# Attention and expert FFN on one core: the attention steps spread over fewer expert tiles

## The chip, the core and the metric

One core of one Trainium2 chip. The metric is the device time of one execution in microseconds; the time before is 1267.89 us, the median of three runs (1267.0 to 1276.63).

## The reference

x has 8 sequences of 1024 tokens with 256 features. After a layernorm two branches are computed from the same xn and both are added to x, all in float32.

```python
xn = layernorm(x)
# causal linear attention, 16 heads of 16
q, k, v = (xn @ W.T split into heads for W in (Wq, Wk, Wv))
q, k = elu(q) + 1, elu(k) + 1
out = einsum('blhd,blhde->blhe', q, cumsum(k (x) v, axis=1))
den = clip(einsum('blhd,blhd->blh', q, cumsum(k, axis=1)), 1e-6)
attention = (out / den).reshape(B, L, 256) @ Wo.T
# mixture of 8 experts, the best 2 for each token
c = softmax over the 2 highest of (xn @ Wr + br), zero elsewhere
ffn = sum over e of c[e] * ((silu(xn @ W1[e]) * (xn @ W3[e])) @ W2[e])   # hidden size 512
return x + attention + ffn
```

## The kernel before

**Attention** works on 16 blocks of 512 tokens, each cut into 4 chunks of 128. `block_steps(t)` is a generator that gives the work of one block in 9 steps, counted from 0: steps 0 to 3 project q, k and v, transpose k, and take the sums for the denominator (`project`; the matmuls den, and at the end eight rden copies on SP's queue); step 4 computes the scores of chunk 0 (`scores`, tile s_ps) and finishes the block before with `attend`; steps 5 to 8 take one chunk each: `carry` and `weigh` (tile o_ps, then oT on DVE) and, for the chunk before, `attend` (the projection a_ps by Wo on PE, and the copy at on ACT). The last block has a tenth step, which finishes its fourth chunk. That makes LAST = 145 steps.

`attend` adds a block's result to out in DRAM with an accumulating DMA on POOL's queue, one of 512 KB for a block (L1001). For the last block there are two (L999): 384 KB with chunks 0 to 2 once the third is copied, and 128 KB with the fourth.

**The experts' FFN** works on 132 tiles of 128 token-and-expert pairs (j from 0 to 131; NM = 132). Tiles 0 to 24 add to acc_d, which is copied into out after tile 26, the others add to out (out_dram in the profile). For each tile:

- `ffn_load` gathers the token rows xg and the table row entry by two indirect DMAs on POOL's queue, five tiles ahead.
- `ffn_norm` (ACT) and `ffn_halves` (DVE) prepare the rows, and `ffn_turn_halves` turns them by a transposing DMA on SP's queue (halfT), `ffn_join` (ACT) makes xgT of it.
- `ffn_weights(j + 2)` loads W1 and W3 of the tile's expert, 2 x 512 KB on SP's queue, into five buffers.
- `ffn_hidden` computes both halves of gu_ps (L1265, PE), the silu on ACT (L1273) and the product hT on DVE (L1276).
- `ffn_out(j - 1)` computes y_ps of the tile before (L1284, PE) and scales it to y on DVE (L1291). The y tiles have five buffers.
- `ffn_store` adds y to out by an indirect accumulating DMA on POOL's queue (L1295).

Every accumulating DMA into out waits for the one before it to land, since the framework keeps writes to the same DRAM tensor in order, and POOL issues them in its own order, the gathers between them.

**What sets the order.** The main loop goes over j. In each turn it first lets `attend_upto(n)` make attention steps until n are made, and then calls `ffn_step(j)`. n grows with j: slowly up to tile 22 (READ), and from there evenly up to the end, so that attention lies between the FFN tiles on PE. `attend_upto` makes one step in a turn, and a further one only if that is step 0, 4 or 8 of a block (TOGETHER). From what is then in program order a scheduler makes each engine's order; the DMAs on SP's queue, and PE's matmuls in the last tile, keep program order.

```python
        else:
            attend_upto(AHEAD + (LAST - 1 - AHEAD) * (j - READ + 1) // (NM - 1 - READ) + j // (NM - 1))
        ffn_step(j, LATE if N1 < j <= N1 + LATE else 0)
```

Here AHEAD = 23 and LAST = 145. At j = 130 the first 144 steps are done, and the last one comes at j = 131.

Of the kernel before, what the change touches and what calls it, by code (L numbers as in the profile page):

```python
# [64 lines left out]
def tile_attention_moe(  # L65
# [33 lines left out]
    NM = NF - NR  # L99
# [46 lines left out]
    def load_x(t, queue):  # L146
        xbs[t] = f_x.tile([P, NCH, H], F32, tag="xb", name=f"xb{t}")
        in_order(queue.dma_start(out=xbs[t], in_=xf[t]))
# [123 lines left out]
    def moments(t, n):  # L272


        def small(name, *shape, dtype=F32):
            return f_two.tile([P, n * NCH, *shape], dtype, tag=name, name=name)

        less, rstd = (tab[:, t * NCH : (t + n) * NCH, w] for w in (1, 2))
        st = small("st", 6)
        mv = small("mv", 2)  # L280
        for c in range(n * NCH):
            nc.vector.bn_stats(st[:, c, :], xbs[t + c // NCH][:, c % NCH, :])
            nc.vector.bn_aggr(mv[:, c, :], st[:, c, :])
        v = small("v")
        nc.vector.tensor_scalar(v, mv[:, :, 1], EPS_NORM, None, ALU.add)
        if t <= FB:
            nc.gpsimd.tensor_tensor(rstd, v, neg_half, ALU.pow)
        else:

            half = small("half")  # L290
            nc.vector.tensor_scalar(half, v, -0.5, None, ALU.mult)
            bits = small("bits", dtype=I32)
            nc.vector.tensor_scalar(bits, v.bitcast(I32), 1, None, ALU.arith_shift_right)
            nc.vector.tensor_scalar(bits, bits, -1.0, float(0x5F3759DF), ALU.mult, ALU.add)
            y = bits.bitcast(F32)
            for i in range(4):
                sq = small("sq")
                nc.vector.tensor_tensor(sq, y, y, ALU.mult)
                nc.vector.tensor_tensor(sq, sq, half, ALU.mult)
                y_new = small(f"y{i % 2}") if i < 3 else rstd  # L300
                nc.vector.scalar_tensor_tensor(y_new, sq, 1.5, y, ALU.add, ALU.mult)
                y = y_new
        yield
        nc.vector.scalar_tensor_tensor(less, mv[:, :, 0], -1.0, rstd, ALU.mult, ALU.mult)
        yield

    def normalise(t):
        xb = xbs.pop(t)
        less, rstd = (tab[:, t * NCH : (t + 1) * NCH, w] for w in (1, 2))
        for c in range(NCH):  # L310
            if t < FB and (c % 2 == 0 or t == FB - 1):
                nc.vector.tensor_scalar(
                    xb[:, c, :], xb[:, c, :], rstd[:, c : c + 1], less[:, c : c + 1],
                    ALU.mult, ALU.add,
                )
            else:
                nc.scalar.activation(
                    xb[:, c, :], xb[:, c, :], AF.Identity, bias=less[:, c : c + 1],
                    scale=rstd[:, c : c + 1],
                )  # L320
        scaled[t] = xb

    def turn(t):
        xn = scaled.pop(t)
        if 0 < t < FB:
            xnT = e_one.tile([P, KC, TB], F32, name=f"xnT{t}")
        else:
            xnT = (two if t == 0 else f_two).tile([P, KC, TB], F32, tag="xnT", name="xnT")
        for k in range(KC):
            tp = ps_t.tile([P, TB], F32, tag="t", name="tp")  # L330
            for c in range(NCH):
                done = nc.tensor.transpose(  # L332
                    tp[:, bass.ts(c, P)], xn[:, c, bass.ts(k, P)], ident
                )
                if t == FB + 1:
                    in_order(done)
            nc.scalar.copy(xnT[:, k, :], tp)
        turned[t] = xnT
        if t == 0:
            turned_first.append(xnT)  # L340
        elif t != FB - 1:
            store(t)
# [19 lines left out]
    def add_logits(t, n, tp):  # L362
        a = t % ROUND
        if a == 0:
            lgs[t] = f_two.tile([P, ROUND * NCH, E], F32, tag="lg_all", name="lg_all")
        nc.vector.tensor_tensor(
            lgs[t - a][:, a * NCH : (a + n) * NCH, :],
            tp.rearrange("p (c e) -> p c e", e=32)[:, :, 0:E],
            br_sb.unsqueeze(1).to_broadcast([P, n * NCH, E]), ALU.add,
        )  # L370
# [664 lines left out]
    LAST = NBLK * STEPS + 1  # L1035
# [11 lines left out]
    def attend_upto(n, apart=True):  # L1047
        first = True
        while steps_made[0] < min(n, LAST):
            if apart and not first and steps_made[0] % STEPS not in TOGETHER:  # L1050
                break
            next(steps)
            steps_made[0] += 1
            first = False
# [117 lines left out]
    def ffn_load(j):  # L1172
        table, _, num_i, src_i, _, _, i = of_tile(j)
        xg[j] = ffn4.tile([P, H], F32, tag="xg", name="xg")
        rows = nc.gpsimd.indirect_dma_start(  # L1175
            out=xg[j], out_offset=None, in_=x_rows[:, :],
            in_offset=bass.IndirectOffsetOnAxis(ap=src_i[:, i : i + 1], axis=0),
        )
        entry[j] = ffn8.tile([P, 3], F32, tag="entry", name="entry")
        nc.gpsimd.indirect_dma_start(  # L1180
            out=entry[j], out_offset=None, in_=table[:, :],
            in_offset=bass.IndirectOffsetOnAxis(ap=num_i[:, i : i + 1], axis=0),
        )
        return rows

    def ffn_norm(j):
        in_order(
            nc.scalar.activation(  # L1188
                xg[j], xg[j], AF.Identity, bias=entry[j][:, 1:2], scale=entry[j][:, 2:3]
            )  # L1190
        )
# [3 lines left out]
    def ffn_halves(j):  # L1195

        halves[j] = ffn2.tile([P, 2, H], U16, tag="half", name="half")
        nc.vector.tensor_copy(  # L1198
            halves[j], xg.pop(j).bitcast(U16).rearrange("p (h b) -> p b h", b=2)
        )  # L1200
# [102 lines left out]
    def ffn_step(j, behind):  # L1303


        while loaded[0] < min(NM, j + (5 if j >= READ else 4)):
            ffn_load(loaded[0])
# [29 lines left out]
    LATE = 3  # L1337
    LISTS = NBLK - FB
    READ = LISTS + 10
    AHEAD = 2 + LISTS // 2 + 3 * (READ - LISTS) // 2  # L1340
    for j in range(NM + 1):
        if j + 1 < TURNED:
            ffn_norm(j + 1)
        if TURNED <= j + 2 < NM:
            ffn_norm(j + 2)
            ffn_halves(j + 2)
        t = FB + j
        counting = FB < t <= NBLK and t % ROUND == 0
        if counting and t == NBLK:
            for _ in routing:  # L1350
                pass
        if 0 < j and t < NBLK:
            if j % 2 == 0:
                with tc.issue_after((last_token if j < 4 else last_masked)[0].ins):
                    for _ in moments(t, 2):
                        pass
            normalise(t)
            turn(t)
            if t + 5 < NBLK:
                load_x(t + 5, nc.scalar)  # L1360
            add_logits(t, 1, logits_turned(t))
            if (t + 1) % ROUND == 0:
                routing = route(t + 1 - ROUND, t + 1)
                next(routing)
        if j == LISTS:
            in_order(
                nc.sync.dma_start(
                    out=tab_d[1][1 : 1 + NS * P, :].rearrange("(p i) w -> p (i w)", p=P),
                    in_=tab.rearrange("p i w -> p (i w)"),
                )  # L1370
            )
            in_order(nc.sync.dma_start(out=tab_d[1][0:1, :], in_=before[0:1, 0:3]))
            lists = second_batch(taken)
        if LISTS <= j < READ:
            next(lists)
        if LISTS <= j < LISTS + NBLK - FB:
            t = FB + j - LISTS
            rows = slice(t * TB, (t + 1) * TB)
            in_order(nc.sync.dma_start(out=out_rows[rows, :], in_=x_rows[rows, :]))
        if j < LISTS:  # L1380
            attend_upto(3 + j // 2)
        elif j < READ:
            attend_upto(AHEAD - 3 * (READ - j - 1) // 2)
        else:
            attend_upto(AHEAD + (LAST - 1 - AHEAD) * (j - READ + 1) // (NM - 1 - READ) + j // (NM - 1))
        ffn_step(j, LATE if N1 < j <= N1 + LATE else 0)
        if counting and j < LISTS:
            for _ in routing:
                pass
        if j == N1 + 1:  # L1390
            copied.append(j)
            in_order(nc.sync.dma_start(out=out_rows[0 : FT * P, :], in_=acc_d[:, :]))
# [54 lines left out]
```

## Time and profile before

| what | value |
|---|---|
| median of three runs | 1267.89 us |
| the profiled execution, its own time | 1267.09 us |
| its span, from the first to the last instruction | 1265.3 us |
| PE (TensorE matmul) busy | 1217.8 us, 96% of the span |
| PEld (TensorE weight load) busy | 1057.0 us, 84% |
| DVE (VectorE) busy | 676.0 us, 53% |
| ACT (ScalarE) busy | 557.1 us, 44% |
| POOL (GpSimd) busy | 519.9 us, 41% |
| moved by DMA | 245.84 MB, 194 GB/s in the mean |
| granted TensorE clock, mean | 0.991 |

PE and PEld are two parts of one engine that overlap. Starts are in microseconds from the begin of the span. A line such as `L1295 POOL DMA_INDIRECT out_dram<-y,dst_i` names the line of the kernel, the engine, the operation, and the tile written from the tiles read; in brackets stands how long the engine had been idle before it, and what that idle time is put down to. For POOL's DMAs the duration is that of the issue, not of the transfer. A wait for several things is put down to the one that came last by the profile, and "issue" means that nothing the profile shows was waited for.

### The profile page before, as it was taken

What the parts mean: (1) busy time and instruction counts of PE and PEld (TensorE: products, weight loads), DVE (VectorE), ACT (ScalarE), POOL (GpSimd) and SP (SyncE); (2) the same over time, 40 slices, a digit from 0 to 9 for tenths busy, and PEclk for the clock granted to TensorE, in tenths of its full rate; (3) what the DMA queues carried; (4) which work ended last, traced back from release to release, by engine and by line L of the source; (5) the groups of instructions that cost most, each with busy time, mean ns of one, the idle gap of its engine ahead of it and who ended that gap; (6) DMA issues with size and microseconds to landing.
All of it is one profiled execution on the core that took longest, in us unless ns stands there. A gap on an engine that the chain in (4) does not pass through costs nothing.

```text
span 1265.3 us, 29694 instructions
## 1 busy us (share of the span) xinstructions
PE 1217.8 (96%) x11434; PEld 1057.0 (84%) x11434; DVE 676.0 (53%) x1541; ACT 557.1 (44%) x1062; POOL 519.9 (41%) x460
## 2 busy tenths in 40 slices
PE   5899999999999999999999999999999999999995
PEld 3577887787898998888888889989888889899884
DVE  7767589863354454545454544545453544545451
ACT  4565465461433526262623426162625344262620
POOL 3643233233344544443435444443544444443422
PEclk9999999999999999999999999999999999999997
DMA  9897565557788697969789897979897787969782
GB/s 329 289 288 242 168 189 119 187 155 208 206 201 194 165 235 164 225 173 211 168 194 203 164 234 155 223 181 192 185 206 171 198 202 170 216 154 231 167 176 35
DMA packets 203678, 245.84 MB, mean 194 GB/s; under 512 B 72674, under 2 KB 127586, under 8 KB 203250
## 3 DMA queue, kind: packets, MB, share of 16 engines
q1 hardware_dynamic: 160146, 189.65, 52.2%
q0 software_dynamic: 38064, 43.27, 24.5%
q10 hardware_dynamic: 5328, 11.01, 2.4%
q8 instruction: 94, 1.54, 0.5%
q14 instruction: 46, 0.38, 0.1%
HBM read 187.91 MB, written 44.29 MB: 184 GB/s over the span
## 4 chain that ended last, share of the span: by engine, by line
PE 86%; DVE 6%; DMA 3%; ACT 2%; issue 1%; POOL 1%; SPq 0%; POOLq 0%; DVEq 0%; ACTq 0%
PE gu_ps L1265 36%; PE y_ps L1284 16%; PE s_ps L911 6%; PE o_ps L948 5%; PE a_ps L990 4%; PE zq L794 4%; PE zkv L810 4%; PE zkk L810 4%; PE o_ps L930 2%; PE tp L332 1%; PE tp L857 1%; DMA halfT<-half 1%; PE lg_ps L355 1%; DVE at_place L572 1%; PE den L879 1%
## 5 line engine op out<-in xcount | busy, mean ns | idle before, releaser
L1265 PE MATMUL gu_ps<-xgT,w 128*128 128x128 f32 x4224 | 507.8, 278 | 1.2 <-DVE s_sb L918 0.8
L1265 PEld LDWEIGHTS gu_ps<-xgT,w 128*128 128x128 f32 x4224 | 488.0, 192 | 19.9 <-issue 13.5
L1295 POOL DMA_INDIRECT out_dram<-y,dst_i x107 | 175.5, 1640 | 338.4 <-DVE y L1291 72.9
L1284 PE MATMUL y_ps<-w_sb,hT 128*128 x1056 | 250.9, 381 | 1.8 <-DVE hT L1276 1.6
L1175 POOL DMA_INDIRECT xg<-in_x_dram,src_i x132 | 128.3, 972 | 230.5 <-DVE half L1198 99.0
L1284 PEld LDWEIGHTS y_ps<-w_sb,hT 128*128 128x128 f32 x1056 | 190.9, 191 | 23.2 <-DVE hT L1276 2.0
L918 DVE TENSOR_TENSOR s_sb<-s_ps,causal 128x512 f32<-128x512 f32 x256 | 159.9, 683 | 86.8 <-PE s_ps L911 76.8
L1273 ACT ACTIVATE hT<-gu_ps 128x512 f32<-128x512 f32 x132 | 78.8, 597 | 284.5 <-PE gu_ps L1265 279.8
L1276 DVE TENSOR_TENSOR hT<-gu_ps,hT 128x512 f32<-128x512 f32 x132 | 90.4, 685 | 64.9 <-PE gu_ps L1265 36.6
L1180 POOL DMA_INDIRECT entry<-tab_d,of_i x107 | 105.9, 990 | 42.3 <-issue 31.7
L1198 DVE COPY half<-xg 128x512 uint16<-128x512 uint16 x105 | 47.9, 457 | 132.4 <-ACT xg L1188 132.4
L1291 DVE TENSOR_SCALAR y<-y_ps,entry 128x256 f32<-128x256 f32 x132 | 63.7, 483 | 101.5 <-PE y_ps L1284 101.4
L995 ACT COPY at<-a_ps 128x256 f32<-128x256 f32 x64 | 23.7, 371 | 169.5 <-PE a_ps L990 127.0
L911 PE MATMUL s_ps<-qm,kT 32*128 32x256 f32 x1024 | 89.0, 405 | 1.7 <-DVE hT L1276 1.6
L1216 ACT COPY xgT<-halfT 128x512 uint16<-128x512 uint16 x105 | 79.7, 760 | 4.9 <-DMA halfT<-half 4.8
L1188 ACT ACTIVATE xg<-xg,entry 128x256 f32<-128x256 f32 x132 | 78.8, 598 | 3.6 <-DMA entry<-tab_d,num_i 3.6
L990 PE MATMUL a_ps<-wo_sb,oT 128*128 128x256 f32 x256 | 68.4, 389 | 3.0 <-DVE oT L965 2.8
L948 PE MATMUL o_ps<-s_sb,va 128*32 128x128 f32 x2048 | 70.7, 278 | 0.0
L911 PEld LDWEIGHTS s_ps<-qm,kT 32*128 32x128 f32 x1024 | 51.8, 184 | 20.9 <-issue 10.7
L948 PEld LDWEIGHTS o_ps<-s_sb,va 128*32 128x32 f32 x2048 | 52.8, 110 | 18.1 <-issue 15.5
L1295 POOL DMA_INDIRECT acc_d<-y,src_i x25 | 41.2, 1649 | 53.1 <-DVE y L1291 18.0
L794 PE MATMUL zq<-xnT,wq_sb 128*128 128x512 f32 x128 | 60.3, 613 | 0.3 <-DVE s_sb L918 0.3
(215 smaller groups left out, 1343.9 us busy)
## 6 DMA issues: line engine op xcount, KB each, us to landing
w<-in_w_dram SPq DMA_DIRECT2D x264, 512.0 KB
rden<-over SPq DMA_DIRECT2D x128, 64.0 KB
xnT_d<-xnT ACTq DMA_DIRECT2D x15, 512.0 KB
xnT<-xnT_d SPq DMA_DIRECT2D x15, 512.0 KB
out_dram<-at POOLq DMA_DIRECT2D x13, 512.0 KB
out_dram<-in_x_dram SPq DMA_DIRECT2D x12, 512.0 KB
xb<-in_x_dram SPq DMA_DIRECT2D x10, 512.0 KB
w_sb<-in_w_dram SPq DMA_DIRECT2D x4, 1024.0 KB
```

Source lines behind the costliest of these rows:

```text
L794: nc.tensor.matmul(z, lhsT=wq_sb[:, k, bass.ts(o, P)], rhs=xnTs[t][:, k, :], start=(k == 0), stop=(k == KC - 1),)
L810: nc.tensor.matmul(z[:, i, :], lhsT=xnTs[t][:, k, bass.ts(c + i, P)], rhs=wkv_sb[:, k, a, :], start=(k == 0), stop=(k == KC - 1),)
L911: nc.tensor.matmul(s_ps[r][:, hh].rearrange("p a l -> p (a l)"), lhsT=kT[rows, hh, span], rhs=qm[rows, hh, :, span], start=True, stop=True,)
L918: last_masked[0] = nc.vector.tensor_tensor(sm, s_ps[r].rearrange("p k a l -> p (k a) l"), causal_b, ALU.mult)
L948: nc.tensor.matmul(o_ps[32 * r : 32 * r + 32, hh, :], lhsT=va[:, c, 4 * hh + r, a, :], rhs=s_sb[r][:, 2 * hh + a, :], start=(first and a = ...
L990: nc.tensor.matmul(a_ps, lhsT=oT[:, hh, :], rhs=wo_sb[:, hh, :], start=(hh == 0), stop=(hh == 1),)
L1175: rows = nc.gpsimd.indirect_dma_start(out=xg[j], out_offset=None, in_=x_rows[:, :], in_offset=bass.IndirectOffsetOnAxis(ap=src_i[:, i : i ...
L1180: nc.gpsimd.indirect_dma_start(out=entry[j], out_offset=None, in_=table[:, :], in_offset=bass.IndirectOffsetOnAxis(ap=num_i[:, i : i + 1], ...
L1265: done = nc.tensor.matmul(ps[:, i, :], lhsT=w13[:, k, bass.ts(i, P)], rhs=xgT[j][:, k, :], start=(k == 0), stop=(k == KC - 1),)
L1276: nc.vector.tensor_tensor(hT, gu[1], hT, ALU.mult)
L1284: done = nc.tensor.matmul(y_ps, lhsT=hT[:, i, :], rhs=w2_sb[:, bass.ds(e * (IC * H) + i * H, H)], start=(i == 0), stop=(i == IC - 1),)
L1295: nc.gpsimd.indirect_dma_start(out=rows[:, :], out_offset=bass.IndirectOffsetOnAxis(ap=dst_i[:, i : i + 1], axis=0), in_=ys.pop(j), in_off ...
```

## The change

The number of attention steps wanted after tile j reaches its end at j = END = 127 instead of 131. The step count for each tile from 22 on is spread over 105 tiles instead of 109. The last step (the fourth chunk of the last block) is due at tile 127 or 128 at the latest; by the counts of the new formula it is made at 127, and tiles 128 to 131 have no attention step. The addition of the last block in two parts (L999) stays as it is.

```diff
     READ = LISTS + 10
+    END = NM - 5
     AHEAD = 2 + LISTS // 2 + 3 * (READ - LISTS) // 2
...
         else:
-            attend_upto(AHEAD + (LAST - 1 - AHEAD) * (j - READ + 1) // (NM - 1 - READ) + j // (NM - 1))
+            spread = (LAST - 1 - AHEAD) * (min(j, END) - READ + 1) // (END - READ)
+            attend_upto(AHEAD + spread + j // (END + 1))
         ffn_step(j, LATE if N1 < j <= N1 + LATE else 0)
```

Tiles up to 28 have the steps that they had. From 29 on a step comes at the same tile or up to four tiles earlier: block 15 begins at tile 120 instead of 123, its weighing of chunk 3 is at tile 126 instead of 130, and its last step at 127 instead of 131.

## The prediction

> **What bounds the kernel now.** I read the page first, then the windows by stage, then the timeline of the end and of POOL alone. The page:
>
> ```profile
> span 1265.3 us, 29694 instructions
> PE 1217.8 (96%) x11434; PEld 1057.0 (84%) x11434; DVE 676.0 (53%) x1541; ACT 557.1 (44%) x1062; POOL 519.9 (41%) x460
> PEclk9999999999999999999999999999999999999997
> ```
>
> The share of 96% is a mean. By stages (columns: window, its length, busy time of PE, PEld, DVE, ACT, POOL, then granted clock, DMA share, GB/s):
>
> ```profile
> 350.00:500.00 150.00, 148.78 (x1392) 132.01 (x1391) 74.50 (x137) 64.16 (x109) 68.00 (x56) 1.00 0.86 195
> 500.00:650.00 150.00, 150.00 (x1425) 132.61 (x1424) 73.06 (x134) 62.62 (x108) 66.43 (x55) 1.00 0.81 186
> 650.00:800.00 150.00, 150.00 (x1459) 134.12 (x1458) 74.03 (x138) 62.78 (x106) 65.73 (x55) 1.00 0.88 196
> 1100.00:1240.00 140.00, 140.00 (x1339) 124.26 (x1338) 67.32 (x124) 58.32 (x98) 51.84 (x41) 1.00 0.77 173
> 1240.00:1250.40 10.40, 9.55 (x59) 8.35 (x57) 2.13 (x4) 0.97 (x2) 2.56 (x2) 1.00 0.39 52
> 1250.40:1265.30 14.90, 0.01 (x1) 0.00 (x0) 0.48 (x1) 0.00 (x0) 3.16 (x2) 0.57 0.23 26
> ```
>
> PE is full from 350 us to 1240 us at clock 1.00 (the windows left out are full as well); the one hole is 1.22 us near 386 us. So where attention stands between the tiles costs nothing there, and moving it gains nothing. Then PE ends at 1250.41 and 14.9 us follow without it. The timeline of the end, all engines, shows what fills them:
>
> ```profile
> 1248.41 2.00 PE L1284 MATMUL y_ps<-w_sb,hT 128*128 x8 [0.85 <-DVE hT L1276]
> 1249.06 0.91 POOL L999 DMA_DIRECT2D out_dram<-at  x1 [2.74 <-DMA out_dram<-y,dst_i]
> 1250.44 0.48 DVE L1291 TENSOR_SCALAR y<-y_ps,entry 128x256 f32<-128x256 f32 x1 [2.09 <-PE y_ps L1284]
> 1253.58 1.62 POOL L1295 DMA_INDIRECT out_dram<-y,dst_i  x1 [3.61 <-DMA out_dram<-at]
> 1258.07 1.54 POOL L1295 DMA_INDIRECT out_dram<-y,dst_i  x1 [2.87 <-DMA out_dram<-y,dst_i]
> ```
>
> Every addition into out_dram waits until the one before it has landed, and they leave in POOL's order. The last tile's y is in memory at 1250.92 but leaves at 1258.07: its turn comes 7.66 us after PE's end. From there to the end of the span it is 7.2 us, whatever happens. The end is set by this chain of additions, not by PE. Further back on POOL:
>
> ```profile
> 1211.98 1.40 POOL L1001 DMA_DIRECT2D out_dram<-at  x1 [4.37 <-DMA out_dram<-y,dst_i]
> 1222.56 1.65 POOL L1295 DMA_INDIRECT out_dram<-y,dst_i  x1 [9.18 <-issue]
> 1227.82 1.55 POOL L1295 DMA_INDIRECT out_dram<-y,dst_i  x1 [3.62 <-DVE kv L977]
> 1232.37 1.56 POOL L1295 DMA_INDIRECT out_dram<-y,dst_i  x1 [2.99 <-DMA out_dram<-y,dst_i]
> 1237.92 1.35 POOL L999 DMA_DIRECT2D out_dram<-at  x1 [4.00 <-issue]
> 1244.67 1.65 POOL L1295 DMA_INDIRECT out_dram<-y,dst_i  x1 [5.40 <-issue]
> ```
>
> Read the starts as steps of the chain. Quiet memory: 128 KB take 4.39, 4.52 and 4.49 us (the three last), 384 KB take 6.75 us (1237.92 to 1244.67). With weights in flight: 128 KB take 5.26 us (1222.56 to 1227.82) or 5.95 us (from the store at 1206.03 to 1211.98), 512 KB take 10.58 us (1211.98 to 1222.56); over all blocks a 512 KB addition takes 8.7 to 13.2 us to the next one.
>
> **The change, part by part.** No instruction is added or removed. Counting the steps out, block 15 moves three to four tiles earlier: its fourth chunk's scores are weighed at tile 126 and its last projection (a_ps) is done ahead of tile 127, where it was in the midst of 131. Earlier blocks slide by 0 to 3 tiles; the first difference is at tile 29.
>
> Middle, tiles 29 to 127: the same PE work in the same order of blocks, its 121 steps spread over 105 tiles instead of 109. In the old run blocks 4 to 6 make steps 3 and 4 apart, blocks 7 to 11 together, and both lie in the windows that are full. Cost 0, covered by PE; DVE at 73 of 150 us and ACT at 64 have room.
>
> At tile 29 two queues are passed. On POOL the addition of block 2 (L1001, 512 KB) now goes ahead of the stores of y 25 and y 26, which went first. The old rows there:
>
> ```profile
> 371.82 1.44 POOL L1001 DMA_DIRECT2D out_dram<-at  x1 [2.29 <-issue]
> 383.69 1.62 POOL L1295 DMA_INDIRECT out_dram<-y,dst_i  x1 [8.44 <-DMA out_dram<-at]
> 390.77 1.80 POOL L1295 DMA_INDIRECT out_dram<-y,dst_i  x1 [4.02 <-DMA out_dram<-y,dst_i]
> ```
>
> L1001 should start near 365 (the old den matmuls at 361.7, then scores and a_ps with 2.3, copy and issue some 1.4), y 25 follow at 365 + 11.9 = 377 and land 7.1 us later, at 384. The y tiles have five buffers, so y 30 on DVE waits for that; it was written at 386.4, so about 2 us are to spare. The gathers queued behind these stores on POOL run five tiles ahead. On SP the load of xnT now follows the rden copies at once, with the weights behind it (0.7 us of issue). Bounds: the hole of 1.22 us goes (-1.2), or y 25 takes 13.2 us behind L1001 and as long as the worst POOL row, and DVE holds PE (+2). I take 0: nearest rows leave it covered.
>
> Tail on PE: tiles 128 to 131 have only their own 3.57 (gu) + 1.73 (y) = 5.3 us. Weights are asked for two tiles ahead (10.6 us), the transposed halves likewise; the shortest old distance from a transposition's issue to its use without a wait is 6.5 us. PE's end E stays at 1250.4: same work, same last wait of 0.85 us.
>
> Tail on POOL: the order becomes three y, 384 KB of block 15, y 125, 128 KB of block 15, y 126 to y 131. From the a_ps of the third chunk to E I add the pieces of the old chain: 0.90 + 0.44 + 1.01 + 1.98 (half of gu 126) + 1.74 (y 125) + 0.86 (a_ps) + 4 x 5.3 + 5.69 (tile 131's gu with y 130 between) + 2.85 (wait and last y) = 36.7 us. The 384 KB left 2.75 us after its a_ps started (1235.17 to 1237.92), so now at E - 33.9. From it to the issue of y 131 there are eight steps: one of 384 KB, seven of 128 KB.
> - Quiet: 6.75 + 7 x 4.47 = 38.0, issue at E + 4.1. Gain 3.6 us.
> - Weights in flight until about E - 15, which covers the first three steps: 384 KB at 9.0 (6.75 x 10.58 / 7.9, where 7.9 is the quiet 512 KB: 4.5 + 3 x 1.13, as 256 KB more cost 6.75 - 4.5), two at 5.6, five at 4.47 = 42.6, issue at E + 8.7. Loss 1.0 us.
> - Heavy: 384 KB at 11.3 (from 13.2), three at 5.95, four at 4.47 = 47.0, issue at E + 13.1. Loss 5.4 us.
>
> I take the middle one, since the old row with weights in flight and the same neighbours is 10.58. So what leaves the end of the queue (two additions of block 15) is replaced by a queue that starts full and drains at 5.3 - 4.47 = 0.83 us a tile: four tiles give back 3.3 us of a backlog of about 12. Sum against the profiled execution of 1267.09 (span 1265.3 and 1.8 around it): 1267.1 + 1.0 + 0 = 1268.1; the median of the runs, 1267.89, lies 0.8 above that execution, which would make 1268.9. I give 1268.5, between the two.
>
> [...]
>
> **The rivals.**
> - Quiet chain: the stores of tiles 122 to 131 find memory as free as the old tail. For it: only six transfers of 512 KB remain. Against it: PE asks for them in 16 us. 1267.9 - 3.6 = 1264.3.
> - Slower chain, on the other side: the 384 KB addition, issued amid weights, takes 11 us and the next three 6 us. For it: 512 KB took 12 to 13 us in five blocks. The eight steps reach the old end at 33.9 + 7.7 = 41.6 us in all; from there each microsecond more is one of loss. 1267.9 + 5.4 = 1273.3.
> - Weights too late: six transfers (3.15 MB) between E - 32 and their last use at E - 4.8 need 118 GB/s; the emptiest old window had 98 by its own low demand. At 98 they end 5.3 us late; the chain hides part of that, so 1273 at most. Against: no gu waits for weights anywhere.
> - Full gain: the steps average 4.3 us and y 131 leaves at E + 0.8: 1267.9 - 6.9 = 1261.0. No 128 KB step that short exists.
> - It does not do what it says: the steps are held apart and attention stays in 128 to 131. The order of instructions excludes it.
>
> **How the numbers follow.** Forecast 0.58, quiet chain 0.2, slower chain 0.12, weights 0.05, full gain 0.05. Low end: quiet chain less the 1.2 of the hole is 1263.1, and 0.6 more for the full gain, 1262.5; high end: slower chain plus 2 us at tile 29, 1275.5 rounded up. About 1% (12.7 us) is what a measurement of this kernel can tell from no change; no case reaches it by itself, so 0.02 faster, 0.94 within, 0.04 slower.
>
> **What would show it.** Right: PE ends at 1250 +- 1.5, POOL issues at equal steps up to the end with no idle wait for y, y 131 leaves 4 to 13 us after PE, six y stores follow the last addition of block 15. Wrong: a gu that waits for DMA after 1220 us, a PE hole of over 2 us near 385 us, or a last store that goes out as soon as its y is there.

## The result, and the profile after

The changed kernel takes 1274.18 us in the median (1264.66 to 1280.68, 20 runs), the kernel before 1268.44 us (1266.17 to 1276.63, 20 runs). The ratio is 1.0036, with a 95% interval of 1.0022 to 1.0049: about 4.6 us slower (the two medians lie 5.7 us apart), less than the 1% within which the prediction called two times the same. The forecast was 1268.5 us; the time lies 5.7 us above it and inside the range.

The profiled execution of the changed kernel took 1274.84 us. First its page: span and instructions, busy time of the engines, and the granted clock in 40 slices.

```profile
span 1273.1 us, 29695 instructions
PE 1219.6 (96%) x11434; PEld 1058.2 (83%) x11434; DVE 674.4 (53%) x1541; ACT 556.9 (44%) x1062; POOL 519.4 (41%) x460
PEclk9899999999999999999999999999999999999997
```

The work is the same, and the share of PE still reads 96%. The loss can't be seen here; the 8 in the clock's second slice lies long before tile 29, the first that differs, and that tile's denominator matmuls start at 361.4 us, where they started at 361.6 before. The windows by stage show it (window, length, busy time of PE, PEld, DVE, ACT and POOL, granted clock, DMA share, GB/s):

```profile
350.00:500.00 150.00, 146.74 (x1362) 129.94 (x1364) 72.48 (x134) 62.80 (x108) 63.48 (x53) 0.99 0.86 189
500.00:650.00 150.00, 148.27 (x1411) 130.81 (x1412) 72.69 (x134) 62.00 (x106) 65.96 (x55) 1.00 0.86 181
...
1100.00:1240.00 140.00, 140.00 (x1353) 126.47 (x1352) 67.52 (x126) 56.78 (x99) 56.21 (x45) 1.00 0.85 192
1240.00:1256.20 16.20, 15.31 (x105) 13.94 (x104) 3.53 (x6) 2.34 (x4) 4.71 (x3) 1.00 0.37 66
1256.20:1273.10 16.90, 0.00 (x0) 0.00 (x0) 0.48 (x1) 0.00 (x0) 4.66 (x3) 0.57 0.21 23
```

Two windows lack PE time: 3.26 us are missing in the first (1.22 before) and 1.73 in the second (none before). All other windows from 650 to 1240 us are full. So there are two losses, one in the middle and one behind PE's end. The timeline of POOL alone, over the end (start, duration of the issue, and in brackets the idle time before it):

```profile
1219.81 1.59 POOL L1295 DMA_INDIRECT out_dram<-y,dst_i  x1 [1.75 <-DVE oT L965]
1224.99 1.41 POOL L999 DMA_DIRECT2D out_dram<-at  x1 [3.60 <-DMA out_dram<-y,dst_i]
1232.05 1.65 POOL L1295 DMA_INDIRECT out_dram<-y,dst_i  x1 [5.65 <-DVE hT L1276]
1236.63 0.94 POOL L999 DMA_DIRECT2D out_dram<-at  x1 [2.93 <-DMA out_dram<-y,dst_i]
1242.98 1.62 POOL L1295 DMA_INDIRECT out_dram<-y,dst_i  x1 [5.42 <-issue]
1247.81 1.54 POOL L1295 DMA_INDIRECT out_dram<-y,dst_i  x1 [3.21 <-DVE hT L1276]
1252.25 1.55 POOL L1295 DMA_INDIRECT out_dram<-y,dst_i  x1 [2.89 <-DVE y L1291]
1256.71 1.55 POOL L1295 DMA_INDIRECT out_dram<-y,dst_i  x1 [2.91 <-DVE y L1291]
1261.20 1.55 POOL L1295 DMA_INDIRECT out_dram<-y,dst_i  x1 [2.95 <-DMA out_dram<-y,dst_i]
1265.66 1.56 POOL L1295 DMA_INDIRECT out_dram<-y,dst_i  x1 [2.91 <-DMA out_dram<-y,dst_i]
```

And all engines at the very end:

```profile
1254.17 1.99 PE L1284 MATMUL y_ps<-w_sb,hT 128*128 x8 [0.85 <-DVE hT L1276]
1256.20 0.48 DVE L1291 TENSOR_SCALAR y<-y_ps,entry 128x256 f32<-128x256 f32 x1 [2.09 <-PE y_ps L1284]
```

PE ends at 1256.16 (1254.17 + 1.99), 5.75 us later than before, and y of tile 131 leaves 9.50 us after that (1265.66), where it was 7.66. Six y stores follow the last addition of block 15, at even steps of 4.4 to 4.8 us. The label "DVE y" at 1252.25 and 1256.71 misleads: by the order of the queue these are y 128 and y 129, which had long been ready; what DVE ended at that moment was another tile. The even step, the same as where the label says DMA, shows that the landing of the addition before is what is waited for.

The sum against the old execution: 5.75 (PE's end) + 1.84 (queue behind it) = 7.6 of the 7.8 us between the two spans. The medians of the runs lie 5.7 apart: this pair of executions shows somewhat more than the typical loss.

**The hole in the middle.** All engines of the changed kernel between 430 and 466 us; of the lines only those of one copy, the addition that it waits for, and what stands behind it:

```profile
433.82 0.37 ACT L995 COPY at<-a_ps 128x256 f32<-128x256 f32 x1 [2.28 <-PE a_ps L990]
438.16 1.62 POOL L1295 DMA_INDIRECT out_dram<-y,dst_i  x1 [1.34 <-DVE half L1198]
444.25 1.45 POOL L1001 DMA_DIRECT2D out_dram<-at  x1 [3.19 <-ACT hT L1273]
446.62 1.03 PE L990 MATMUL a_ps<-wo_sb,oT 128*128 128x256 f32 x4
458.64 0.37 ACT L995 COPY at<-a_ps 128x256 f32<-128x256 f32 x1 [13.62 <-DMA out_dram<-at]
458.91 0.60 ACT L1273 ACTIVATE hT<-gu_ps 128x512 f32<-128x512 f32 x1
459.07 1.42 PE L990 MATMUL a_ps<-wo_sb,oT 128*128 128x256 f32 x4 [3.26 <-ACT at L995]
461.27 2.33 PE L911 MATMUL s_ps<-qm,kT 32*128 32x256 f32 x16
```

The same place in the kernel before:

```profile
441.23 0.37 ACT L995 COPY at<-a_ps 128x256 f32<-128x256 f32 x1 [3.94 <-PE a_ps L990]
445.05 1.42 POOL L1001 DMA_DIRECT2D out_dram<-at  x1 [2.28 <-ACT xg L1188]
454.04 1.03 PE L990 MATMUL a_ps<-wo_sb,oT 128*128 128x256 f32 x4
455.74 0.37 ACT L995 COPY at<-a_ps 128x256 f32<-128x256 f32 x1 [2.36 <-DMA out_dram<-at]
463.05 1.03 PE L990 MATMUL a_ps<-wo_sb,oT 128*128 128x256 f32 x4
```

Read it so. Block 3's fourth copy (433.82; before 441.23) comes a tile earlier, 7.4 us. Its addition L1001 doesn't: it stands in POOL's order behind two y stores, whose chain hardly moved, and leaves at 444.25 instead of 445.05. The next block's first a_ps is earlier again by 7.4 us (446.62; before 454.04). Its copy needs the at tile, of which there is one buffer, and that is free only when L1001 has been read out. Before, the copy's input was ready at 455.07 (454.04 + 1.03) and it started 0.67 us later. Now the input is ready at 447.65 and the copy starts 11.0 us later. The silu of the FFN tile stands behind that copy on ACT: it starts 8.67 us after its gu (450.24 to 458.91), where the one before it took 2.09 us (441.22 to 443.31). PE is held more directly: a_ps and y_ps take turns in two result buffers (the pool ps_y), so its next a_ps needs the one that this copy empties. PE had work until 455.81 and waits for the copy for 3.26 us.

The earlier order alone doesn't make the hole. From the issue of L1001 to the start of the copy it is 10.7 us before (445.05 to 455.74) and 14.4 us after (444.25 to 458.64). PE goes on 0.43 us after the copy starts (458.64 to 459.07), so after the change all beyond 11.1 us (455.81 - 0.43 - 444.25) is a hole: with the old 10.7 us there would have been none. Before, PE came back for that buffer only at 463.05 and didn't wait, so by the same count up to 6.9 us were to spare. The new order used up this slack, and a longer transfer in this execution made the hole. Why the transfer took longer is open.

The chain of work that ended last, in order of time, now runs through that transfer at this place, and later through one transposition of halves. In the kernel before no addition of at is in the chain ahead of the end:

```profile
444.25 14.29 DMA out_dram<-at
581.17 10.64 DMA halfT<-half
```

The second hole (1.73 us at 592.5) is of that other kind: ACT waits 4.22 us for halfT there, whose transposition took 10.64 us, and DVE's hT and PE wait behind it. The kernel before has one hole of that kind, its 1.22 us near 386, where halfT took 11.34 us. In both kernels the late transposition was issued within 1 us of a block's 512 KB addition. Before, L1001 starts at 371.82 and the transposition at 372.79; after:

```profile
581.17 1.39 SPq L1207 DMA_TRANSPOSE halfT<-half  x1
581.78 1.41 POOL L1001 DMA_DIRECT2D out_dram<-at  x1 [2.67 <-DMA out_dram<-y,dst_i]
```

So the additions of attention stand beside both kinds of hole. That they delay each other is an argument; no run moved one away from the other. Behind the first hole the clock falls as well, as the windows of one microsecond show:

```profile
460.00:461.00 1.00, 1.00 (x6) 0.91 (x4) 0.35 (x1) 0.90 (x3) 0.95 (x1) 0.50 1.06 389
462.00:463.00 1.00, 1.00 (x15) 0.90 (x10) 0.15 (x1) 0.00 (x0) 0.69 (x2) 0.50 0.83 138
464.00:465.00 1.00, 1.00 (x43) 0.96 (x34) 1.00 (x3) 0.00 (x0) 0.75 (x1) 1.00 0.52 148
```

That is why s_ps takes 2.33 us at 461.27 where it took 1.15 at 448.03. PE reads as busy in this stretch (10.00 of 10 us from 460 to 470, at a clock of 0.84), so this loss is in no "idle" column; as lost clock over windows of 10 us it is 1.7 us. PE's end is thus 5.75 later by holes (3.26 + 1.73 - 1.22 = 3.8), clock (1.7), and some 0.3 that is left over.

### The profile page after: what moved, and what is told of

Same layout as the page of the kernel before. It is cut to its first block, busy times and chain, and to the rows that moved or that the text cites. A ratio compares the mean times of both kernels' runs of the same rounds, so it can differ in the third digit from the quotient of the medians.

```text
span 1273.1 us, 29695 instructions
## 1 busy us (share of the span) xinstructions
PE 1219.6 (96%) x11434; PEld 1058.2 (83%) x11434; DVE 674.4 (53%) x1541; ACT 556.9 (44%) x1062; POOL 519.4 (41%) x460
## 4 chain that ended last, share of the span: by engine, by line
PE 85%; DMA 5%; DVE 4%; ACT 2%; SPq 1%; issue 1%; POOL 0%; POOLq 0%; ACTq 0%; DVEq 0%
PE gu_ps L1265 36%; PE y_ps L1284 16%; PE s_ps L911 6%; PE o_ps L948 5%; PE a_ps L990 5%; PE zkv L810 4%; PE zq L794 4%; PE zkk L810 4%; PE o_ps L930 2%; DMA out_dram<-at 1%; DMA out_dram<-y,dst_i 1%; PE tp L857 1%; DMA acc_d<-in_x_dram 1%; DMA halfT<-half 1%; PE tp L332 1%
## 5 line engine op out<-in xcount | busy, mean ns | idle before, releaser
L990 PEld LDWEIGHTS a_ps<-wo_sb,oT 128*128 128x128 f32 x256 | 46.1, 190 | 18.0 <-issue 4.3
```

The costliest lines, as they stand in the source:

```text
L990: nc.tensor.matmul(a_ps, lhsT=oT[:, hh, :], rhs=wo_sb[:, hh, :], start=(hh == 0), stop=(hh == 1),)
```

## The experiments

They ran in three sets, each with runs of the kernel before beside it, on three chips: there the kernel before takes 1291.32 us (35 runs), 1288.63 (29) and 1268.86 (23). Only on the last do the times agree with those of the result, so ratios are compared within a set alone. Two measures are worked out from each trace: G, from PE's end to the start of the last y store, and M, from the denominator matmuls of tile 29 (the first tile that the change touches) to PE's end.

| kernel | set | median us | ratio [95%] | G us | M us |
|---|---|---|---|---|---|
| before | result | 1268.44 | 1 | 7.66 | 888.8 |
| after | result | 1274.18 | 1.0036 [1.0022, 1.0049] | 9.50 | 894.7 |
| a_at5 | 1 | 1290.84 | 1.0008 [0.998, 1.0036] | 9.71 | 897.0 |
| b_at5 | 1 | 1289.16 | 0.9984 [0.9961, 1.0007] | 8.10 | 905.1 |
| mid_only | 1 | 1293.01 | 1.0029 [1.0004, 1.0055] | 7.71 | 902.9 |
| tail_only | 1 | 1293.29 | 1.0012 [0.9994, 1.0031] | 13.67 | 900.8 |
| after_2 | 2 | 1292.14 | 1.0011 [0.9981, 1.0041] | 9.47 | 895.5 |
| a_at5_2 | 2 | 1290.2 | 0.9995 [0.9962, 1.0028] | 12.66 | 897.3 |
| a_at5_one | 2 | 1290.36 | 1.0004 [0.9974, 1.0034] | 7.82 | 896.6 |
| a_at5_no15 | 2 | 1286.8 (one run) | none | 3.31 | 901.1 |
| before_2 | 3 | 1269.24 (one run) | none | 8.27 | 888.0 |
| after_3 | 3 | 1273.99 (one run) | none | 9.91 | 893.6 |
| a_at5_end12 | 3 | 1273.23 | 1.0027 [1.0009, 1.0044] | 13.36 | 889.1 |
| a_at5_end3 | 3 | 1265.97 | 0.9974 [0.9956, 0.9992] | 9.31 | 886.7 |

The theory: the middle loses because the one at tile is wanted again before its addition has gone; the end loses because the queue of additions is no shorter. The rival for the middle: nothing there but chance, and all of the loss at the end.

**More buffers for at (a_at5, b_at5).** The at tiles of blocks 3 to 15 come from a pool with five buffers that is idle by then; the order of instructions on every engine stays. a_at5 does this to the changed kernel, b_at5 to the kernel before.

```diff
-            ats[t] = one.tile([P, NCH, H], F32, tag="at", name=f"at{t}")
+            ats[t] = (f_x if t > 2 else one).tile([P, NCH, H], F32, tag="xb" if t > 2 else "at", name=f"at{t}")
```

> The changed kernel, with the tile at of blocks 3 to 15 in a pool of five buffers instead of one; the order of every engine is the same. Theory A (the one at buffer): in the changed kernel ACT waits up to 13.6 us at its at copy until the block before has been added into out, the silu behind it is late, PE has a hole of 3.3 us near 456 us and then some 10 us at a clock of 0.84. Without that wait PE ends about 5 us earlier: 1268 to 1270 us, no wait of ACT for out_dram<-at, last y store still 8 to 10 us after PE's end. Theory B (the queue of additions at the end holds all of the loss): the same as the changed kernel, 1273 to 1275 us. Theory C (DMA is too full in the middle wherever it strikes): the hole turns up elsewhere, 1271 to 1275 us.

> The kernel before, with the same five buffers for at. Theory A: in the kernel before ACT waits for the additions too (34.3 us in all, at most 6.3 at once) but PE never does, so within 1 us of the kernel before. Theory C: the same. If it gains 3 us or more, the one buffer cost PE something in the kernel before that its profile does not show.

Measured: the wait of ACT on the addition of at is gone from both traces altogether (not one entry in the list of ACT's waits). With five buffers in both, the old pace is 0.0024 better in ratio than the changed one (0.9984 against 1.0008); G, 8.10 against 9.71, makes 1.6 us or 0.0012 of that. On this chip tile 29's start and many small holes all over vary by several microseconds between kernels, there is no trace of the kernel before from it, and the two traces are of unlike executions (1287.61 us for a_at5, under its median; 1295.75 us for b_at5, above it). M is higher for b_at5 than for a_at5, against the ratios, so M says nothing here. The ratios fit the theory, but their intervals overlap and leave room for no gain, so they don't decide.

**Middle alone and tail alone (mid_only, tail_only).** The new pace up to tile 106 and the old count from there, or the reverse.

```diff
-            attend_upto(AHEAD + spread + j // (END + 1))
+            if j < 107:     # tail_only: j >= 107
+                attend_upto(AHEAD + spread + j // (END + 1))
+            else:
+                attend_upto(AHEAD + (LAST - 1 - AHEAD) * (j - READ + 1) // (NM - 1 - READ) + j // (NM - 1))
```

> Half of the change: attention as in the changed kernel up to tile 106, from 107 on the old count of steps, so that tiles 107 to 109 have no attention step and the end is as in the kernel before. Theory A: the hole near 456 us is here as well, PE ends 4 to 6 us late, the last y store leaves 7.7 us after PE's end as before: 1271 to 1274 us. Theory B: the end is the old one, so 1267 to 1269 us.

> The other half: attention as in the kernel before up to tile 106, then the new count, which is caught up with at tile 120; tiles 128 to 131 without attention. Theory A: no hole near 456 us, PE's end within 1.5 us of the kernel before, the last y store 9 to 10 us after it: 1269 to 1271 us. Theory B: all of the loss is here, 1272 to 1275 us.

Measured: 1.0029 for the middle, whose interval leaves out 1, and 1.0012 for the tail; together 1.0041, beside the 1.0036 of the whole. The middle costs something even where the end is the old one (G 7.71). But its trace has no hole at the at copy (ACT's longest wait for it is 5.9 us); its one large hole, 2.51 us at 1090, has no releaser in the trace. And tail_only has a G of 13.67, not that of the whole change: it has to catch up within the tiles from 107 to 120, and its steps in the queue are 5.4 to 8.0 us long up to 1269.6 us. So the two don't divide the change cleanly, and the place of the middle's loss isn't the same on this chip.

**The change once more, and with five buffers, side by side (after_2, a_at5_2).**

> The changed kernel once more, unaltered, so that it stands beside the next ones on one chip. Theory A (the one at buffer holds ACT in the middle, and PE with it): 1.003 to 1.006 of the kernel before, with ACT waits for out_dram<-at of over 6 us and a PE hole behind at least one of them. Theory C (DMA is too full in the middle, the place is chance): the same ratio, holes without such a wait.

> The changed kernel with five buffers for at, once more. Theory A: 0.002 to 0.005 below the changed kernel of this call (3 to 6 us). Theory C: within 0.0015 of it.

Measured: five buffers are 0.0016 better (0.9995 against 1.0011), with intervals of ±0.003: inconclusive. In this trace of the changed kernel ACT's longest wait for at is 6.89 us and PE has no hole behind it, so the hole that the theory expected here is missing. The addition took 12.2 us up to the copy (447.09 to 459.31), but it left 6.9 us ahead of the a_ps that this copy empties (447.09 to 454.02), where it was 2.4 us in the first trace (444.25 to 446.62) and 9.0 in the kernel before. Nor was the loss of the whole change (1.0011) clear on this chip.

**The last block in one part (a_at5_one), and not at all (a_at5_no15).** Both with five buffers. In one part, 512 KB leave after the fourth chunk; in the other kernel block 15's additions are left out.

```diff
-        if t == NBLK - 1 and c >= NCH - 2:
+        if t == NBLK - 1 and c >= NCH:     # a_at5_one alone
...
-            nc.gpsimd.dma_start(out=to[t][:, some, :], in_=at[:, some, :], accum_op=ALU.add)
+            pass     # a_at5_no15 alone
```

> As a_at5, with the last block added in one part of 512 KB once its fourth chunk is copied, instead of 384 and 128 KB: one addition less in the queue that sets the end. By the steps of the changed kernel's trace (7.1, 4.6 and 6.4 us for 384 KB, y, 128 KB; 10 us for 512 KB, which can start 2 to 6 us later): the last y store leaves 7 to 9 us after PE's end instead of 9.5, a gain of 1 to 2 us on a_at5. If the queue did not set the end, nothing would change.

> As a_at5, with the additions of the last block (block 15's attention) into out left out: those 512 rows lack their attention. It takes two steps, some 11.5 us, out of the queue. If the queue alone sets the end, the last y store leaves as soon as its y is there, 0.5 to 1.5 us after PE's end instead of 9.5, and nothing else changes. If the y stores alone keep the queue full, it stays at 3 us or more.

The end of a_at5_one on POOL:

```profile
1239.09 1.40 POOL L1001 DMA_DIRECT2D out_dram<-at  x1 [2.83 <-ACT xg L1188]
1248.82 1.65 POOL L1295 DMA_INDIRECT out_dram<-y,dst_i  x1 [8.33 <-issue]
```

One step of 9.73 us replaces two (in the changed kernel 384 KB took 7.06 and 128 KB 6.35), and G is 7.82, within what was expected. In the ratios no gain shows: 1.0004 against 0.9995 for a_at5_2, with intervals of ±0.003. Without block 15's additions G is still 3.31, where an empty queue would give 0.5 us, as an estimate from the scaling of y in the changed kernel (PE ends at 1256.16, DVE at 1256.68; y 129 to 131 would leave when DVE has them). So on this chip the y stores alone keep the queue from running empty at the end, and finishing attention earlier can't empty it.

**The pair once more, on a chip as quick as that of the result (before_2, after_3).**

> The kernel before, unaltered, for a trace from the chip that the others of this call run on. From the den matmuls of block 3 (tile 29) to PE's end it took 888.8 us in the first trace, with 2.1 us of idle PE. If that stretch is the same on every chip, 888 to 890 us; if chance collisions in DMA decide it, 892 to 905 us. The last y store leaves 7.5 to 8.2 us after PE's end either way.

> The changed kernel, unaltered, for a third trace. The same stretch took 894.7 and 895.5 us in its first two. Theory A (the one at buffer costs PE time in most executions): an ACT wait of over 8 us for out_dram<-at with a PE hole of over 1 us right behind it. Theory C (chance): longest wait under 8 us and no hole behind it. The last y store 9.4 to 10 us after PE's end, up to 13 where the weights of the last tiles are in the way.

Measured: M 888.0 and 893.6, so the 5.9 us between the first two traces come back as 5.6. The timeline of after_3 at the place of the hole:

```profile
444.41 1.42 POOL L1001 DMA_DIRECT2D out_dram<-at  x1 [3.50 <-ACT hT L1273]
446.54 1.03 PE L990 MATMUL a_ps<-wo_sb,oT 128*128 128x256 f32 x4
456.70 0.37 ACT L995 COPY at<-a_ps 128x256 f32<-128x256 f32 x1 [11.78 <-DMA out_dram<-at]
457.13 1.13 PE L990 MATMUL a_ps<-wo_sb,oT 128*128 128x256 f32 x4 [1.41 <-ACT at L995]
```

The same copy waits, at the same tile, for the same addition, as the theory had it. It starts 12.3 us after L1001 here (444.41 to 456.70) instead of 14.4, and PE's hole is 1.41 us (and 0.53 us right behind it). A second hole, 1.40 us near 1000, again follows a late halfT (issued at 988.76, next to L1001 at 989.06; ACT waits 3.90 us for it, up to 998.97), and this time the clock falls behind that one. before_2 has no hole over 0.6 us but the last wait of 0.85, though the same addition took 12.75 us up to the next copy there (447.19 to 459.94): longer than in after_3, and covered. G of before_2 is 8.27, a little above what was expected.

**Where attention ends (a_at5_end12, a_at5_end3).** Five buffers, and END at tile 120 or 129 instead of 127.

```diff
-    END = NM - 5
+    END = NM - 12     # a_at5_end3: NM - 3
```

> As a_at5, with attention spread to tile 120 instead of 127, so that 11 tiles stand alone. The last block is added some 37 us earlier. If a store takes 4.5 us even there, the queue is empty well before the end and the last y store leaves 1 us after PE's end: 8 us less than a_at5. If it takes 5.3 to 6 us as long as weights flow, the queue does not drain before the last three tiles, 6 to 10 us after PE's end. If 1 MB of weights every 5.3 us is more than DMA gives, PE has holes of over 1 us at gu between tile 121 and 131, and the sum is above a_at5.

> As a_at5, with attention spread to tile 129 instead of 127, half way back to the kernel before. By the count of steps in the queue the last y store leaves 8 to 9 us after PE's end, between 7.7 (to tile 131) and 9.5 (to tile 127); a_at5 less 0 to 1.5 us.

In both there is no wait for at, and M is 889.1 and 886.7, at the level of the kernel before: in these two traces the loss in the middle is gone (one hole of 1.33 us is left in a_at5_end12, near 774). Two windows of a_at5_end3, for the two that were not full:

```profile
350.00:500.00 150.00, 150.00 (x1420) 133.59 (x1422) 74.30 (x139) 64.52 (x111) 66.22 (x55) 1.00 0.88 196
500.00:650.00 150.00, 150.00 (x1466) 133.67 (x1459) 75.05 (x139) 61.45 (x104) 65.55 (x54) 1.00 0.84 186
```

What is left in a_at5_end12 is the end. Its eleven lone tiles keep PE full, but on POOL the y stores take longer steps while weights stream in (the window gives the traffic of all DMA, 259 GB/s):

```profile
1190.00:1220.00 30.00, 30.00 (x233) 28.97 (x232) 8.20 (x16) 10.25 (x18) 14.95 (x13) 1.00 1.09 259
```

```profile
1205.62 1.63 POOL L1295 DMA_INDIRECT out_dram<-y,dst_i  x1 [3.55 <-DVE hT L1276]
1210.46 1.63 POOL L1295 DMA_INDIRECT out_dram<-y,dst_i  x1 [0.68 <-DVE half L1198]
1217.50 1.62 POOL L1295 DMA_INDIRECT out_dram<-y,dst_i  x1 [2.87 <-DVE y L1291]
1223.74 1.62 POOL L1295 DMA_INDIRECT out_dram<-y,dst_i  x1 [2.08 <-issue]
1230.44 1.58 POOL L1295 DMA_INDIRECT out_dram<-y,dst_i  x1 [3.79 <-DMA out_dram<-y,dst_i]
```

Steps of 4.84, 7.04, 6.24 and 6.70 us for 128 KB, while a lone tile brings a new y every 5.3 us: the queue grows while it should drain, and G becomes 13.36, where at most 10 was expected. The fewer lone tiles, the less of that. a_at5_end3, with two, is 0.9974 of the kernel before (0.9956 to 0.9992), some 3.3 us faster than it, and has the lowest median and ratio of all; its G is 9.31, a little over the 8 to 9 that were expected. How much of its gain is due to the buffers and how much to the two lone tiles wasn't told apart: b_at5, which has the buffers alone, is 0.9984 on another chip.

## Why the prediction was right or wrong

- **The sum came out as "the same", for a reason that holds only in part.** Both losses are below 1%. The rivals "slower chain" (1273.3) and "weights too late" (1273 at most) lie nearer to the median than the forecast does; but the steps of the chain were not slower than forecast and no gu waited for weights, so being near is no evidence for them. That the time is inside the range is luck in part: the top of the range was set by a slower chain, not by a PE that ends late. Two figures of the second rival are off without consequence: six transfers in 27.2 us are 116 GB/s, not 118, and at 98 GB/s they end 4.9 us late, not 5.3.
- **The step that failed** is "Middle, tiles 29 to 127: ... Cost 0, covered by PE", and with it "PE's end E stays at 1250.4". E was 1256.16, outside the ±1.5 that was named as a sign. The full windows of the old run show that PE was covered then; they don't show how near the cover was to its end. The old trace did: the list of ACT's waits of the kernel before has this line (in total, times, longest, in us):

```profile
ACT at L995 <- DMA out_dram<-at: 34.3, 8, 6.0
```

  and that of the changed kernel this one:

```profile
ACT at L995 <- DMA out_dram<-at: 35.8, 6, 13.6
```

  The wait was there, eight times, hidden by the PE work queued ahead. The total hardly changed; the longest one more than doubled and came out from under its cover. What the runs showed in place of the 0 is 5.75 us: 3.26 of this hole, 1.73 of the other, 1.7 of lost clock and some 0.3 unexplained, less the old hole of 1.22. The prediction priced PE's time and DVE's and ACT's room, but not this wait for a single buffer, though it knew that the change moves attention past the y stores on POOL. It worked that through at tile 29 only, where the first difference is, and not where block 4 follows block 3.
- **Tile 29** went as reckoned: L1001 was put near 365 and started at 365.15, y 25 was put at 377 and left at 373.36, and no hole is near 385: the old one of 1.22 us went, which was the lower of the bounds named there, where 0 was taken. On POOL of the changed kernel:

```profile
365.15 1.44 POOL L1001 DMA_DIRECT2D out_dram<-at  x1 [5.35 <-ACT at L995]
373.36 1.62 POOL L1295 DMA_INDIRECT out_dram<-y,dst_i  x1 [3.59 <-DMA out_dram<-at]
```

- **The tail on PE** was right: no gu waits for weights, and the last wait is again 0.85 us.
- **The tail on POOL** was right in mechanism and sign, and a little too small: a loss of 1.0 us was forecast, 1.84 measured. Two terms were off, in opposite directions. The 384 KB were to leave at E - 33.9 and left at E - 31.2, because y 124, issued at 1219.81, was still landing. The eight steps were to take 42.6 us and took 40.7 (1224.99 to 1265.66): 7.06 for the 384 KB, 4.58 and 6.35 while weights flow, then 4.83 and four of about 4.46.
- **The quiet chain and the full gain** needed the queue to drain. a_at5_no15 shows that on its chip it doesn't, even with block 15's additions gone (one execution; its steps from 1238.08 to 1273.45 are 5.0 to 7.3 us). On a chip like that of the result this wasn't run. By the steps of the changed kernel's trace, its two additions of block 15 are 13.4 us of the queue (7.06 + 6.35) and y 131 waits for 9.0 us (9.50 - 0.5), so there, as an estimate, the queue would have drained without them. No step at the ends of the runs here is below 3.8 us (a_at5_end3, 1239.05 to 1242.85).
- **The stretch of FFN alone** costs PE nothing: even the eleven lone tiles of a_at5_end12 keep it full (30.00 of 30 us from 1190 to 1220). It costs in the queue of additions, as the same run shows (G 13.36).

What is shown and what isn't: the hole behind the at copy is seen in two executions on the chips where the kernel before takes some 1268 us, at the same tile; the wait vanishes with five buffers, and M returns to the old level in two such kernels, though with another END. The size of that hole hangs on the length of one transfer: 3.26 us of hole at 14.4 us, 1.41 at 12.3 and, by the count above, none at the old 10.7. END at 127 with five buffers wasn't run on such a chip. The hole itself is 1.9 to 3.3 us of the 5.6 to 5.9 in M; the lost clock (1.7 us in both) and what the holes behind a late halfT add to those of the kernel before (1.73 us against 1.22, and 1.40 against 0.47) make up most of the rest. Why a transposition is late at one place and not at another is open. On the two other chips this loss could not be separated from their scatter.

## What to carry to other kernels

A wait for a single buffer, with other work queued behind it on the same engine, may cost nothing today (here up to 6.0 us, covered) and still be the first thing to break when work is moved (13.6 us, with a PE hole of 3.26 us): read its longest case and the slack behind it, at every place where the order shifts, not at the first only. At an end set by a chain of accumulating DMAs, count the steps and what each costs under load; finishing other work earlier helps only if the chain then drains faster than new work arrives (in a_at5_end12 it took 4.84 to 7.04 us a step while a new y came every 5.3 us, and G grew to 13.36). A share of 96% busy can hide a loss of 5 us, and a window full of PE work a slower clock (0.84 from 460 to 470); compare the holes and the clock in windows of a few microseconds.

## What the runs showed of the hardware

- After a PE hole of 3.26 us (after, 455.81 to 459.07) the granted clock was 0.50 from about 460 to 463 us; in after_3 a hole of 1.40 us (near 1000) was followed by 0.50 to 0.55 from 1003 to 1006, and in b_at5 one of 1.45 us (near 397) by a mean of 0.97 from 390 to 400 and of 0.86 from 400 to 410, while holes of 1.73 us (after, 592), 1.41 us (after_3, 456) and 2.51 us (mid_only, 1090) were followed by none. So in these runs a hole's length alone doesn't decide; what does wasn't shown.
- A dependent addition of 128 KB takes a step of about 4.5 us near and behind PE's end (after, 1252.25 to 1265.66: 4.46, 4.49 and 4.46, where DMA moves 23 GB/s in all from 1256.2 on), and 4.8 to 7.0 us at the end of a_at5_end12 while weights come in (259 GB/s over all DMA from 1190 to 1220 us).
- A late transposing DMA stood beside a 512 KB accumulating one: three that left PE idle for over 1 us on chips where the kernel before takes some 1268 us (before near 386, after near 592, after_3 near 1000) were issued within 1 us of it and took 11.34, 10.64 and 10.2 us. Not every such pair makes a hole: the kernel before has one (583.02 and 583.62) whose halves were in use 6.59 us after the issue, without a wait.
- The same kernel takes 1268.86, 1288.63 and 1291.32 us on three chips: a spread of 1.8%, about five times the effect that was looked for. These sets ran at different times too, so it isn't shown that the chip is the cause.
